# A graph-attention layer on one core: shared adjacency and key buffers, weight-row terms as columns, five x buffers

## The chip, the cores and the metric

The kernel runs on one core of a Trainium2 chip. It is one program: TensorE (PE in the profile), VectorE (DVE), ScalarE (ACT), GpSimd (POOL) and SyncE (SP, which here only issues DMAs) each run their own list of instructions in order and wait for each other through semaphores. The metric is the device time of one execution in microseconds (us). Lower is better.

## The reference

The inputs are x (3327 rows of 1024 fp32), a symmetric 0/1 matrix adj (3327 x 3327, int32, with ones on the diagonal, some 0.5% of its entries set), weights Wf, Wg, W (1024 x 1024) and biases bf, bg, bW (1024, zeros in this data but computed with).

```python
h = jnp.maximum(_layernorm(x, axis=-1), 0.0)
f = h @ Wf + bf
g = h @ Wg + bg
e = jax.nn.relu(f @ g.T)
scores = jnp.where(adj > 0, e, NEG)
attention = jax.nn.softmax(scores, axis=1)
out = x + attention @ (h @ W + bW)
```

(The reference's lines, with the inner function written in place.) Only the scores at the entries of adj that are set matter.

## The kernel before, in words

The kernel works on edges instead of the full matrix (function `edge_path`). If a row turns out to have too many edges, it falls back on a dense version (`dense_path`), which doesn't run on this data.

It uses e(i, j) = relu(q(i) · h(j) + q(i, D)), where q = h A + v, A = Wf Wg^T, v is the row bf Wg^T, column D of A is Wf bg, and element D of v is bf · bg. All of A, v and bW3 must be there before the second part can end its first product.

**Part 1** (L369 to L606) loops over 26 tiles of 128 rows (the last has 127). For each tile t:

- `degrees(t)` loads 128 rows of adj into `a` (1.7 MB, sync queue, L446), takes Relu on ACT with the row sum as degree (L448) into `r`, and multiplies `r` by the column number on POOL (L449). `a` and `r` have two buffers each (L376, L377), of 13.3 KB in each partition.
- `normed(t)` loads x (L417, sync queue, buffer `xt` from a pool of three, L374), computes mean and variance (on DVE for odd t, on ACT for even t), normalizes, takes Relu on ACT (L438) and stores h to a DRAM table `hd` (L440, ACT's queue).
- `edges(t, r)` finds the column numbers of the set entries on DVE: sixteen max8 instructions over segments of r (L458), then five more max8 with replacement (L465, L467), and writes the list and the degree to `pay`. PE counts degrees in a running histogram `pre` (L476, L481), from which DVE reads the rank of each row among those of its degree (`hit`, L478).
- for t below 8, `load_Wg(t)` loads 128 rows of Wg and transposes them on PE (L498, L499) into WgT; for t from 8 to 15, `make_A(t - 8)` loads rows of Wf, transposes them, and multiplies them with WgT on PE (L525, 32 instructions for each c), with copies out of PSUM on ACT (L528) and one column for Wf bg (L531, L532).

After the loop, rows are ranked by degree (L562 to L600), which gives `perm`: row numbers in order of falling degree. Then `make_rows` (L601) computes v on PE as rows of three equal copies (L543, from bf3, three copies of bf as columns), and `split3` turns v, and bW loaded three times as a row (`bWf`), into three bf16 terms that sum to it, one in each of three partitions. It does so on DVE over [3, 512] tiles: for each of the five pieces a copy (L355), three roundings (L359), three multiplications with a row of the 3 x 3 identity `sel3` (L361, L363), two subtractions (L365) and a copy (L366). The results v3 and bW3 are added later by a bf16 product with `ones3`.

**Part 2** goes through the 26 tiles of sorted rows. `prepare(s)` gathers the lists (`pi`) and h rows (`hp`) by perm (POOL queue, L627), transposes hp on PE (L638), and computes q on PE (L655, with v3 added in L656) and ACT (L657). `dot` gathers one neighbour row G of hd for each of 128 rows and dots it with q on DVE (L672); `softmax`, `combine` (L729 to L735) and `project` (L749, with bW3 added in L750) follow, and `finish` scatters the result. The G buffers, W_sb (4 MB, L610), pi and others use SBUF memory that part 1 gives back.

The order of instructions on each engine and queue isn't the program's. A planner orders them when the program is built, by its own estimates of durations, by the order of the program as a priority, and by when a buffer comes free. On the chip each engine keeps to that order and waits.

Of the kernel before, what the change touches and what calls it, by code (L numbers as in the profile page):

```python
# [8 lines left out]
FP = mybir.dt.float32  # L9
I32 = mybir.dt.int32  # L10
AF = mybir.ActivationFunctionType
ALU = mybir.AluOpType
# [7 lines left out]
BF = mybir.dt.bfloat16  # L20
SEG = 16
# [267 lines left out]
def edge_path(ctx: ExitStack, tc: tile.TileContext, x, adj, Wf, bf, Wg, bg, W, bW, out, flag):  # L289
# [10 lines left out]
    nc = tc.nc  # L300
    N, D = x.shape
    O = W.shape[1]
    P = 128
    CB = 512
    KD = D // P
    QB = 342
    QW = 3 * QB
    NT = (N + P - 1) // P
    OH = O // CB
    SW = -(-N // SEG)  # L310
    PW = KM + 1

    def rows(t):
        return min(P, N - t * P)

    def pieces(t):

        n = rows(t)
        m = n - n % 16
        return [(0, m), (m, n - m)] if 0 < m < n else [(0, n)]  # L320

    const = ctx.enter_context(tc.tile_pool(name="const", bufs=1))
# [5 lines left out]
    ident = const.tile([P, P], FP, name="ident")  # L328
# [4 lines left out]
    nc.gpsimd.iota(iotak, pattern=[[1, KM]], base=0, channel_multiplier=0, allow_small_or_imprecise_dtypes=True)  # L333
    ones3 = const.tile([3, P], BF, name="ones3")
    nc.gpsimd.memset(ones3, 1.0)
    sel3 = const.tile([3, 3], FP, name="sel3")
    make_identity(nc, sel3)
    bads = const.tile([P, NT + 2], FP, name="bads")
    nc.gpsimd.memset(bads, 0.0)

# [5 lines left out]
    v3 = wts.tile([3, QW], BF, name="v3")  # L346
    nc.gpsimd.memset(A_sb[:, :, D:], 0.0)
    nc.gpsimd.memset(v3[:, D:], 0.0)
    bW3 = wts.tile([3, O], BF, name="bW3")

    def split3(pool, to, of):

        n = of.shape[1]
        rest = pool.tile([3, n], FP, name="rest")
        tc.keep_in_program_order(nc.vector.tensor_copy(rest, of))  # L355
        part = pool.tile([3, n], BF, name="part")
        acc = pool.tile([3, n], FP, name="part_acc")
        for i in range(3):
            nc.vector.tensor_copy(part, rest)  # L359
            if i == 0:  # L360
                nc.vector.tensor_scalar(acc, part, sel3[:, 0:1], None, op0=ALU.mult)  # L361
            else:
                nc.vector.scalar_tensor_tensor(acc, part, sel3[:, i : i + 1], acc, op0=ALU.mult, op1=ALU.add)  # L363
            if i < 2:
                nc.vector.tensor_sub(rest, rest, part)  # L365
        nc.vector.tensor_copy(to, acc)  # L366


    with ExitStack() as part1:  # L369
        pool1 = lambda name, bufs, **kw: part1.enter_context(tc.tile_pool(name=name, bufs=bufs, **kw))  # L370
        c1 = pool1("c1", 1)
        wrow = pool1("wrow", 2)
        wT = pool1("wT", 2)
        ln = pool1("ln", 3)  # L374
        lnj = pool1("lnj", 1)
        apool = pool1("adj", 2)  # L376
        kpool = pool1("key", 2)  # L377
        cpool = pool1("cand", 2)
        p_tr = pool1("p_tr", 2, space=PSUM)
        p_mm = pool1("p_mm", 2, space=PSUM)  # L380
        p_u = pool1("p_u", 1, space=PSUM)
# [3 lines left out]
        iotaj = c1.tile([P, N], FP, name="iotaj")  # L385
# [6 lines left out]
        part = c1.tile([P, 1], FP, name="part_no")  # L392
# [6 lines left out]
        nc.gpsimd.memset(onesd, 1.0)  # L399
        pay = c1.tile([P, NT, PW], I32, name="pay")  # L400
        deg = c1.tile([P, NT], FP, name="deg")
        cnt = c1.tile([P, NT], FP, name="cnt")
        rp = c1.tile([P, NT], FP, name="rp")
        oh = c1.tile([P, NT, NBIN], BF, name="oh")
# [36 lines left out]

        def degrees(t):
            n = rows(t)
            a = apool.tile([P, N], I32, name="a")
            for b, m in pieces(t):
                nc.sync.dma_start(a[b : b + m], adj[t * P + b : t * P + b + m, :])  # L446
            r = kpool.tile([P, N], FP, name="r")
            nc.scalar.activation(r[:n], a[:n], AF.Relu, accum_out=deg[:n, t : t + 1])  # L448
            nc.gpsimd.tensor_mul(r[:n], r[:n], iotaj[:n])  # L449
            return r  # L450

        def edges(t, r):
# [30 lines left out]
        def store_lists(t0, t1):  # L483
            full = min(t1, N // P)
            if full > t0:
                nc.scalar.dma_start(
                    pd[t0 * P : full * P, :].rearrange("(t p) k -> p t k", p=P), pay[:, t0:full, :]
                )
            if t1 > full:
                for b, m in pieces(full):  # L490
                    nc.scalar.dma_start(pd[full * P + b : full * P + b + m, :], pay[b : b + m, full, :])

        def transposed(to, of):

            for g in range(0, KD, 4):
                ps = p_tr.tile([P, 4, P], FP, name="ps_tr")
                for k in range(4):
                    nc.tensor.transpose(ps[:, k, :], of[:, (g + k) * P : (g + k + 1) * P], ident)  # L498
                nc.scalar.copy(to[:, g : g + 4, :], ps)  # L499

        WgT = c1.tile([P, KD, D], FP, name="WgT")
        bfT = c1.tile([P, KD], FP, name="bfT")
        bgT = c1.tile([P, KD], FP, name="bgT")
        bf3 = c1.tile([P, KD, 3], FP, name="bf3")
        bWf = c1.tile([3, O], FP, name="bWf")
        nc.gpsimd.dma_start(bfT, bf.rearrange("(k p) -> p k", p=P))
        nc.gpsimd.dma_start(bgT, bg.rearrange("(k p) -> p k", p=P))
        nc.gpsimd.dma_start(bWf, bass.AP(tensor=bW.tensor, offset=bW.offset, ap=[[0, 3], [1, O]]))
        nc.vector.tensor_copy(bf3, bfT[:, :, None].to_broadcast([P, KD, 3]))

        def load_Wg(c):
            wr = wrow.tile([P, D], FP, name="wr")
            nc.sync.dma_start(wr, Wg[c * P : (c + 1) * P, :])
            transposed(WgT[:, :, c * P : (c + 1) * P], wr)

        def make_A(c):

            wr = wrow.tile([P, D], FP, name="wr")
            nc.sync.dma_start(wr, Wf[c * P : (c + 1) * P, :])
            WfT = wT.tile([P, KD, P], FP, name="WfT")  # L520
            transposed(WfT, wr)
            for o in range(OH):
                ps = p_mm.tile([P, CB], FP, name="ps_A")
                for k in range(KD):
                    nc.tensor.matmul(  # L525
                        ps, WfT[:, k, :], WgT[:, k, o * CB : (o + 1) * CB], start=(k == 0), stop=(k == KD - 1)
                    )
                nc.scalar.copy(A_sb[:, c, o * CB : (o + 1) * CB], ps)  # L528
            ps = p_u.tile([P, P], FP, name="ps_u")
            for k in range(KD):  # L530
                nc.tensor.matmul(ps[:, 0:1], WfT[:, k, :], bgT[:, k : k + 1], start=(k == 0), stop=(k == KD - 1))  # L531
            nc.scalar.copy(A_sb[:, c, D : D + 1], ps[:, 0:1])  # L532

        def make_rows():

            ps = p_u.tile([P, P], FP, name="ps_u")
            for k in range(KD):
                nc.tensor.matmul(ps[:3, 0:1], bf3[:, k, :], bgT[:, k : k + 1], start=(k == 0), stop=(k == KD - 1))
            split3(c1, v3[:, D : D + 1], ps[:3, 0:1])
            for o in range(OH):  # L540
                ps = p_mm.tile([P, CB], FP, name="ps_A")
                for k in range(KD):
                    nc.tensor.matmul(  # L543
                        ps[:3], bf3[:, k, :], WgT[:, k, o * CB : (o + 1) * CB], start=(k == 0), stop=(k == KD - 1)
                    )
                split3(c1, v3[:, o * CB : (o + 1) * CB], ps[:3])
                split3(c1, bW3[:, o * CB : (o + 1) * CB], bWf[:, o * CB : (o + 1) * CB])

        for t in range(NT):
            r = degrees(t)  # L550
            normed(t)
            edges(t, r)
            if t % 4 == 3 and t > 4:
                store_lists(t - 7, t - 3)
            if t < KD:
                load_Wg(t)
            elif t < 2 * KD:
                make_A(t - KD)
        store_lists(20, NT)


# [27 lines left out]
        ps = p_u.tile([P, P], FP, name="ps_u")  # L589
        for t in range(NT):  # L590
            nc.tensor.matmul(
                ps[:, : 2 * NT], ohp[:, t, :], place[:, t, :, :].rearrange("p a s -> p (a s)"),
                start=(t == 0), stop=(t == NT - 1),
# [4 lines left out]
        over = c1.tile([P, 1], FP, name="over")  # L598
        nc.vector.tensor_scalar(over, part, float(rows(NT - 1)), float(N), op0=ALU.is_ge, op1=ALU.mult)
        nc.vector.tensor_tensor(final, perm[:, NT - 1 : NT], over, op=ALU.add)  # L600
        make_rows()  # L601
        ne = c1.tile([P, NT], FP, name="ne")
        nc.vector.tensor_tensor(ne, deg, cnt, op=ALU.not_equal)
        nc.vector.tensor_reduce(bads[:, NT : NT + 1], ne, AX.X, ALU.max)
# [176 lines left out]
    for s, cap in enumerate(CAPS):  # L781
        half = (cap + 1) // 2
# [11 lines left out]
    for i, (s, k0, k1) in enumerate(units):  # L794
# [5 lines left out]
        if i + 1 < len(units):  # L800
            s2, a, b = units[i + 1]
# [12 lines left out]
def kernel(tc: tile.TileContext, x, adj, Wf, bf, Wg, bg, W, bW, out):  # L814

    nc = tc.nc
    with tc.tile_pool(name="flag", bufs=1) as fpool:
        flag = fpool.tile([1, 1], I32, name="flag")  # L820
        bad = edge_path(tc, x, adj, Wf, bf, Wg, bg, W, bW, out, flag)
        with tc.If(bad > 0):
            dense_path(tc, x, adj, Wf, bf, Wg, bg, W, bW, out)
# [27 lines left out]
```

## Time and profile before

| what | us |
|---|---|
| median of 3 runs | 1439.14 (1438.37 to 1440.06) |
| the profiled execution | 1437.97 |
| its span, first to last instruction | 1436.2 |
| busy in the span: DVE | 1266.7 (88%) |
| PE, matmuls | 1160.7 (81%) |
| POOL | 873.6 (61%) |
| ACT | 442.7 (31%) |

The mean granted TensorE clock was 0.927 of full speed, and DMA moved 259 GB/s on average. Times in the profile are counted from the start of the span. A busy share is an average over stages with different limits, so stages have to be looked at one by one. L12 is line 12 of the kernel. A line with `A <- B` in a list of waits says that A's engine stood idle until B ended. A line of the timeline has the start, the duration, the engine, the line, the operation, what is written and read, and, in square brackets, how long the engine was idle before it and who ended that.

### The profile page before, as it was taken

How to read it: one execution, taken by the hardware profiler on the slowest of the kernel's cores; microseconds unless marked ns; L12 is line 12 of the kernel's file. 1: busy time of each engine (PE TensorE's matmuls, PEld its weight loads, DVE VectorE, ACT ScalarE, POOL GpSimd, SP SyncE). 2: the span in 40 equal slices, each digit the busy share in tenths (PEclk: the TensorE clock that was granted, in tenths of full speed). 3: DMA queues.
4: the chain of work that ended last, by engine and by line, in shares of the span. 5: the costliest groups of instructions: out<-in, count | busy, mean ns of one | idle time of the engine just before them, and what ended most of it. 6: DMA issues, size and time to landing. Idle time of an engine off the chain costs nothing.

```text
span 1436.2 us, 13878 instructions
## 1 busy us (share of the span) xinstructions
PE 1160.7 (81%) x4242; PEld 657.3 (46%) x4242; DVE 1266.7 (88%) x2647; ACT 442.7 (31%) x673; POOL 873.6 (61%) x627
## 2 busy tenths in 40 slices
PE   1249899457087998999979888999999998999676
PEld 1225454034063665556455444555555554555332
DVE  3878888977979999998988889999999988999991
ACT  6666757301060444324122221222222111111100
POOL 8676776426756677665575556666676765666500
PEclk9999899769588999999989898999999998999788
DMA  8898887249768888896796668887787776787700
GB/s 340 292 348 294 325 302 260 86 140 402 236 224 310 310 315 276 302 314 206 279 324 210 230 261 281 292 286 271 266 287 258 257 254 228 252 275 256 263 30 32
DMA packets 97709, 372.51 MB, mean 259 GB/s; under 512 B 14265, under 2 KB 14681, under 8 KB 94297
## 3 DMA queue, kind: packets, MB, share of 16 engines
q0 software_dynamic: 79552, 286.86, 57.6%
q1 hardware_dynamic: 10860, 70.49, 13.4%
q10 hardware_dynamic: 7212, 14.18, 2.6%
q8 instruction: 35, 0.57, 0.2%
q14 instruction: 50, 0.41, 0.1%
HBM read 343.68 MB, written 27.80 MB: 259 GB/s over the span
## 4 chain that ended last, share of the span: by engine, by line
PE 35%; DVE 27%; issue 18%; POOL 10%; DMA 6%; ACT 3%; POOLq 0%; ACTq 0%; SPq 0%; DVEq 0%
PE ps_o L749 16%; DVE y L735 12%; PE ps_q L655 10%; POOL r L449 6%; DVE junk L672 5%; PE yT_ps L713 5%; DMA G<-hd,pi 4%; POOL G L627 4%; DVE cand L458 3%; PE ps_A L525 2%; ACT r L448 1%; PE ps_A L543 1%; DVE xp L757 1%; DVE sc L672 1%; DVE lst L465 1%
## 5 line engine op out<-in xcount | busy, mean ns | idle before, releaser
L627 POOL DMA_INDIRECT G<-hd,pi x468 | 560.8, 1198 | 316.6 <-ACT y L733 99.1
L672 DVE CUSTOM_DVE_ANT_0 junk<-G,q 128x1024 bf16<-128x1024 f32 x468 | 600.7, 1284 | 31.5 <-DMA G<-hd,pi 28.8
L655 PE MATMUL ps_q<-A_sb,hT 128*128 128x342 f32 x1248 | 394.5, 466 | 63.5 <-ACT q L657 53.5
L735 DVE SCALAR_TENSOR_TENSOR y<-G,sc,y 128x1024 f32<-128x1024 f32 x320 | 411.3, 1285 | 4.7 <-ACT y L733 2.9
L749 PE MATMUL ps_o<-W_sb,yT 128*128 128x512 f32 x832 | 387.1, 620 | 9.8 <-ACT yT L744 9.5
L655 PEld LDWEIGHTS ps_q<-A_sb,hT 128*128 128x128 f32 x1248 | 233.2, 194 | 183.4 <-ACT q L657 55.6
L749 PEld LDWEIGHTS ps_o<-W_sb,yT 128*128 128x128 f32 x832 | 161.0, 198 | 207.9 <-issue 189.1
L449 POOL TENSOR_TENSOR r<-r,iotaj 128x3327 f32<-128x3327 f32 (+1 forms) x26 | 187.8, 7232 | 73.1 <-ACT r L448 61.5
L458 DVE MAX8 cand<-r 128x8 f32<-128x208 f32 (+2 forms) x416 | 134.1, 361 | 39.8 <-POOL r L449 39.8
L657 ACT COPY q<-ps_q 128x342 f32<-128x342 f32 x78 | 32.8, 449 | 328.7 <-DVE sc L672 225.2
L729 ACT ACTIVATE G<-G,sc 128x1024 f32<-128x1024 f32 x122 | 129.0, 1136 | 0.0
L525 PE MATMUL ps_A<-WgT,WfT 128*128 128x512 f32 x256 | 120.3, 630 | 2.9 <-ACT WfT L499 2.9
L713 PE MATMUL yT_ps<-ident,G 128*128 128x128 f32 x976 | 116.4, 275 | 1.3 <-ACT G L729 1.3
L713 PEld LDWEIGHTS yT_ps<-ident,G 128*128 128x128 f32 x976 | 106.7, 141 | 13.2 <-ACT G L729 5.9
L639 ACT COPY hT<-ps_t 128x512 f32<-128x512 f32 x52 | 30.1, 593 | 192.1 <-PE ps_q L655 159.8
L744 ACT COPY yT<-yT_ps 128x512 f32<-128x512 f32 x52 | 27.8, 586 | 199.1 <-PE yT_ps L713 199.1
L525 PEld LDWEIGHTS ps_A<-WgT,WfT 128*128 128x128 f32 x256 | 50.8, 202 | 74.1 <-issue 64.7
L448 ACT ACTIVATE r<-a 128x3327 f32<-128x3327 int32 (+1 forms) x26 | 77.2, 2968 | 9.5 <-issue 5.4
L713 PE MATMUL yT_ps<-ident,y 128*128 128x128 f32 x208 | 33.8, 316 | 56.6 <-DVE y L735 35.7
L758 POOL DMA_INDIRECT out_dram<-xp,perm x25 | 31.7, 1268 | 56.9 <-DVE xp L757 50.9
L757 DVE TENSOR_TENSOR xp<-ps_o,xp 128x512 f32<-128x512 f32 x52 | 35.6, 685 | 34.2 <-PE ps_o L750 34.0
L713 PEld LDWEIGHTS yT_ps<-ident,y 128*128 128x128 f32 x208 | 28.0, 163 | 61.4 <-DVE y L735 38.5
(137 smaller groups left out, 748.7 us busy)
## 6 DMA issues: line engine op xcount, KB each, us to landing
a<-in_adj_dram SPq DMA_DIRECT2D x25, 1663.5 KB, 9.1
xt<-in_x_dram SPq DMA_DIRECT2D x25, 512.0 KB, 4.2
hd<-xt ACTq DMA_DIRECT2D x25, 512.0 KB, 5.6
G<-hd,pi POOLq DMA_INDIRECT x468, 6.1
wr<-in_L_gnn_Wg_dram SPq DMA_DIRECT2D x8, 512.0 KB, 6.0
wr<-in_L_gnn_Wf_dram SPq DMA_DIRECT2D x8, 512.0 KB, 5.0
W_sb<-in_L_gnn_W_dram SPq DMA_DIRECT2D x1, 4096.0 KB, 14.2
a<-in_adj_dram SPq DMA_DIRECT2D x1, 1455.6 KB, 9.6
```

Of the source, the lines that this page charges most:

```text
L448: nc.scalar.activation(r[:n], a[:n], AF.Relu, accum_out=deg[:n, t : t + 1])
L449: nc.gpsimd.tensor_mul(r[:n], r[:n], iotaj[:n])
L458: nc.vector.max(cand[:n, s * 8 : s * 8 + 8], r[:n, s * SW : min(N, (s + 1) * SW)])
L525: nc.tensor.matmul(ps, WfT[:, k, :], WgT[:, k, o * CB : (o + 1) * CB], start=(k == 0), stop=(k == KD - 1))
L627: nc.gpsimd.indirect_dma_start(out=to, out_offset=None, in_=table, in_offset=bass.IndirectOffsetOnAxis(ap=idx, axis=0),)
L655: nc.tensor.matmul(ps[:, :QB], hT[:, k, :], A_sb[:, k, o : o + QB], start=(k == 0), stop=False)
L672: nc.vector.tensor_tensor_reduce(junk, g, e["q"][:, :D], 1.0, e["q"][:, D : D + 1], op0=ALU.mult, op1=ALU.add, accum_out=e["sc"][:, k : k ...
L713: nc.tensor.matmul(e["yT"][:, c, :], g[:, c * P : (c + 1) * P], ident, is_transpose=True, start=(first and c % 4 == 0), stop=(last and c % ...
L729: nc.scalar.activation(g, g, AF.Copy, scale=p)
L735: nc.vector.scalar_tensor_tensor(y, g, p, y, op0=ALU.mult, op1=ALU.add)
L749: nc.tensor.matmul(ps, yT[:, k, :], W_sb[:, k, o * CB : (o + 1) * CB], start=(k == 0), stop=False)
L757: nc.vector.tensor_add(xo, e["o"][o], xo)
```

## The change

There are five edits.

1. `a` and `r` become one tile: adj is loaded as int32 into a tile `r` of a pool with four buffers, Relu on ACT works in place (the same bytes read as int32 and written as fp32), and the product on POOL follows in place.
2. For the last two tiles Relu and the product work on the columns in two parts, with the second row sum in `half`, added by an Identity on ACT.
3. `split3`, `sel3`, `bf3` and `bWf` go. v is computed as eight columns of 128 (WgT chunks as the stationary operand, bf as a moving column), bW is loaded as eight columns of 128, and bf · bg makes a seventeenth. They are split into three bf16 terms as a [128, 17] tile on DVE, and PE turns each column's three terms into a three-partition row by a product with a bf16 identity (16 products of 128 columns and one of one column). ACT copies the rows out of PSUM.
4. `make_rows` is called inside the loop, after the tile t = 9 and its make_A, not after the ranking.
5. The pool of `xt` (and its small tiles) has five buffers instead of three.

```diff
-        ln = pool1("ln", 3)
+        ln = pool1("ln", 5)
...
-        apool = pool1("adj", 2)
-        kpool = pool1("key", 2)
+        kpool = pool1("key", 4)
...
         def degrees(t):
             n = rows(t)
-            a = apool.tile([P, N], I32, name="a")
+            r = kpool.tile([P, N], FP, name="r")
+            a = r.bitcast(I32)
             for b, m in pieces(t):
                 nc.sync.dma_start(a[b : b + m], adj[t * P + b : t * P + b + m, :])
-            r = kpool.tile([P, N], FP, name="r")
-            nc.scalar.activation(r[:n], a[:n], AF.Relu, accum_out=deg[:n, t : t + 1])
-            nc.gpsimd.tensor_mul(r[:n], r[:n], iotaj[:n])
+
+            cuts = [0, SEG // 2 * SW, N] if t >= NT - 2 else [0, N]
+            for i, (b, e) in enumerate(zip(cuts, cuts[1:])):
+                to = deg[:n, t : t + 1] if not i else half[:n]
+                nc.scalar.activation(r[:n, b:e], a[:n, b:e], AF.Relu, accum_out=to)
+                nc.gpsimd.tensor_mul(r[:n, b:e], r[:n, b:e], iotaj[:n, b:e])
+                if i:
+                    nc.scalar.activation(deg[:n, t : t + 1], deg[:n, t : t + 1], AF.Identity, bias=half[:n])
             return r
...
-        bf3 = c1.tile([P, KD, 3], FP, name="bf3")
-        bWf = c1.tile([3, O], FP, name="bWf")
+        cols = c1.tile([P, 2 * KD + 1], FP, name="cols")
+        terms = c1.tile([P, 3, 2 * KD + 1], BF, name="terms")
+        identb = c1.tile([P, P], BF, name="identb")
+        nc.vector.tensor_copy(identb, ident)
+        nc.gpsimd.memset(cols, 0.0)
...
-        nc.gpsimd.dma_start(bWf, bass.AP(tensor=bW.tensor, offset=bW.offset, ap=[[0, 3], [1, O]]))
-        nc.vector.tensor_copy(bf3, bfT[:, :, None].to_broadcast([P, KD, 3]))
+        nc.gpsimd.dma_start(cols[:, KD : 2 * KD], bW.rearrange("(k p) -> p k", p=P))
...
         def make_rows():
             ps = p_u.tile([P, P], FP, name="ps_u")
-            ...
+            for c in range(KD):
                 for k in range(KD):
                     nc.tensor.matmul(
+                        ps[:, c : c + 1], WgT[:, k, c * P : (c + 1) * P], bfT[:, k : k + 1],
+                        start=(k == 0), stop=(k == KD - 1),
                     )
+            for k in range(KD):
+                nc.tensor.matmul(ps[0:1, KD : KD + 1], bfT[:, k : k + 1], bgT[:, k : k + 1], start=(k == 0), stop=(k == KD - 1))
+            nc.scalar.copy(cols[:, :KD], ps[:, :KD])
+            nc.scalar.copy(cols[0:1, 2 * KD :], ps[0:1, KD : KD + 1])
+            for i in range(3):
+                nc.vector.tensor_copy(terms[:, i, :], cols)
+                if i < 2:
+                    nc.vector.tensor_sub(cols, cols, terms[:, i, :])
+            for row, first in ((v3, 0), (bW3, KD)):
+                for o in range(OH):
+                    ps = p_mm.tile([P, CB], FP, name="ps_A")
+                    for k in range(CB // P):
+                        c = first + o * (CB // P) + k
+                        nc.tensor.matmul(ps[:3, k * P : (k + 1) * P], terms[:, :, c], identb, start=True, stop=True)
+                    nc.scalar.copy(row[:, o * CB : (o + 1) * CB], ps[:3])
+            ps = p_u.tile([P, P], FP, name="ps_u")
+            nc.tensor.matmul(ps[:3, 0:1], terms[:, :, 2 * KD], identb[:, 0:1], start=True, stop=True)
+            nc.scalar.copy(v3[:, D : D + 1], ps[:3, 0:1])
 
         for t in range(NT):
...
             elif t < 2 * KD:
                 make_A(t - KD)
+            if t == KD + 1:
+                make_rows()
         store_lists(20, NT)
...
-        make_rows()
```

More of the change, by code (lines that the diff above doesn't have):

```diff
@@ L335, in edge_path @@
     nc.gpsimd.memset(ones3, 1.0)
-    sel3 = const.tile([3, 3], FP, name="sel3")
-    make_identity(nc, sel3)
     bads = const.tile([P, NT + 2], FP, name="bads")
@@ L349, in edge_path @@
     bW3 = wts.tile([3, O], BF, name="bW3")
[L351 to L366, printed above, removed]
     with ExitStack() as part1:
@@ L401, in edge_path @@
         deg = c1.tile([P, NT], FP, name="deg")
+        half = c1.tile([P, 1], FP, name="half")
         cnt = c1.tile([P, NT], FP, name="cnt")
@@ L536, in make_rows @@
             ps = p_u.tile([P, P], FP, name="ps_u")
[L537 to L541, printed above, removed]
+            for c in range(KD):
                 for k in range(KD):
                     nc.tensor.matmul(
-                        ps[:3], bf3[:, k, :], WgT[:, k, o * CB : (o + 1) * CB], start=(k == 0), stop=(k == KD - 1)
-                    )
-                split3(c1, v3[:, o * CB : (o + 1) * CB], ps[:3])
-                split3(c1, bW3[:, o * CB : (o + 1) * CB], bWf[:, o * CB : (o + 1) * CB])
+                        ps[:, c : c + 1], WgT[:, k, c * P : (c + 1) * P], bfT[:, k : k + 1],
+                        start=(k == 0), stop=(k == KD - 1),
+                    )
+            for k in range(KD):
[16 more added lines that the diff above has]
+            nc.scalar.copy(v3[:, D : D + 1], ps[:3, 0:1])
         for t in range(NT):
```

## The prediction

> **What bounds the kernel now.** The span by stages comes first (columns: us, busy us of PE, PEld, DVE, ACT, POOL with counts, clock, DMA share, GB/s). The stages are mine: weights Wg (0 to 93), the eight make_A (93 to 250), last tiles, ranking, hand-over, main part.
>
> ```profile
> core 0: us, PE busy (x) PEld busy (x) DVE busy (x) ACT busy (x) POOL busy (x), PEclk, DMA share, GB/s
> 0.00:93.00 93.00, 20.20 (x86) 15.92 (x87) 62.80 (x306) 60.67 (x86) 68.11 (x38) 1.00 0.87 326
> 93.00:250.00 157.00, 142.05 (x466) 73.69 (x466) 126.67 (x628) 105.67 (x160) 111.32 (x16) 0.96 0.81 299
> 250.00:277.00 27.00, 18.30 (x44) 3.09 (x43) 22.11 (x109) 12.67 (x22) 16.56 (x3) 0.80 0.41 119
> 277.00:291.00 14.00, 1.60 (x31) 1.28 (x31) 12.59 (x34) 0.00 (x0) 0.00 (x0) 0.50 0.06 18
> 291.00:330.00 39.00, 25.22 (x99) 15.95 (x98) 24.11 (x60) 3.58 (x7) 14.18 (x15) 0.75 0.56 203
> 330.00:1436.00 1106.00, 953.36 (x3522) 547.40 (x3521) 1018.38 (x1513) 260.11 (x400) 663.43 (x558) 0.93 0.74 257
> ```
>
> The main part is VectorE's: 1018 of 1106 us. The change doesn't touch it, so what comes before it moves the end one for one. Before it no engine is full, except PE from 93 to 250, with 142 of 157. So I asked for the waits of the first 330 us (total us, times, longest), the sync queue's own and then all.
>
> ```profile
> SPq L417 <- DMA hd<-xt: 147.3, 18, 15.9
> SPq L610 <- DMA pd<-pay: 32.6, 1, 32.6
> SPq L610 <- DVE bW L366: 24.7, 1, 24.7
> ```
>
> ```profile
> POOL r L449 <- ACT r L448: 61.5, 18, 8.1
> ...
> ACT nmr L437 <- DVE rstd L436: 30.1, 11, 4.7
> ```
>
> The sync queue stood 147 us because a load of x wanted one of three buffers whose store to hd had not landed; adj and weight loads stood behind it. POOL waited 61 us for ACT's Relu, which itself stood behind small statistics that wait on DVE. The timeline shows the hand-over.
>
> ```profile
> 291.63 1.08 POOL L627 DMA_INDIRECT hp<-hd,perm  x1 [21.90 <-DVE rest L355]
> ...
> 304.95 1.94 PE L638 MATMUL ps_t<-ident,hp 128*128 128x128 f32 x8 [13.49 <-DVE rest L355]
> ...
> 306.76 6.84 PE L655 MATMUL ps_q<-A_sb,hT 128*128 128x342 f32 x16
> ...
> 315.58 0.95 POOL L627 DMA_INDIRECT pi<-pd,perm  x1 [7.13 <-DVE bW L366]
> ...
> 323.97 0.45 ACT L657 COPY q<-ps_q 128x342 f32<-128x342 f32 x1 [4.60 <-PE ps_q L656]
> ...
> 329.88 1.28 DVE L672 CUSTOM_DVE_ANT_0 junk<-G,q 128x1024 bf16<-128x1024 f32 x1 [5.93 <-DMA G<-hd,pi]
> ```
>
> perm is known at 290.8 (L597 runs from 290.59 for 0.18), yet split3 holds DVE from 291.5 to 315.3. PE's first transposes wait for its last read of PSUM (rest L355), the lists (pi) and W_sb for its end. The first dot starts 39.1 us after perm.
>
> **What the Trainium skill says.** "TensorE: Matmul & The Clock Gate", Architectural detail: ACT and DVE are strict FIFO, PE reorders only weight loads; the ACT wait above agrees. Same page, What's actually happening: an idle PE runs at half clock for its first few us; the first 16 matmuls of q took 6.84 us here, the next 4.87. "DMA: Bandwidth & Descriptors", Issuing engines are not separate DMA queues: all queues share 16 engines, so earlier W_sb competes with the gathers; with W_sb under way, gathered G took 8.8 us to land in the first 330 us against 6.1 over the span. "ScalarE: Activation LUTs", Table sets: cheap functions such as identity are in every set; so the new Identity should load no table. The trace has loads for Sqrt at 15.4 and Exp at 342.2 and none between, though Relu, Copy and Square run there; it has no Identity.
>
> **The change, part by part.**
> *split3 leaves the hand-over.* Removed from DVE: 291.5 to 315.3, 23.8 us. What is late next? hp is issued at perm plus 0.9, or 2.1 if a pi goes first (1.25 each); landing 4.8 (median of its three); transposes to first q matmul 1.8 (304.95 to 306.76); q to its last copy 17.7 (306.76 to 324.42). Sum 25.2 to 26.4; W_sb's 4 MB beside it may add up to 6 us, a warm PE may take 2 off. I take 26. G is not later: pi lands after about 6 (5.8), G is issued then and takes 8.8: 16 to 17. By the first dot, 7 or more lie ready, so the 1.1 us gap after the first dot goes too. Gain 39.1 - 26 + 1 = **14 us** (bounds 8 to 16).
> *make_rows at t = 9.* PE loses L543, 17.4 us, and L538, 0.55, all but 0.26 of it after 249.7, beside the last tiles. It gains 8 x 8 column products, each two instructions: L531 makes 16 in 1.84, so 128 take 14.7; bf·bg 0.55 to 1.84; 17 one-pass bf16 products at 0.1 to 0.24 (L476 takes 0.19 to 0.24), 2 to 4. Sum 17 to 21, now ahead of make_A(2) on PE and in p_u and p_mm. ACT gains three copies at 0.16 and four at 0.56, 2.7 us; DVE three casts and two subtracts of 17 columns at about 0.17, 0.85, and one 128x128 cast. The handing over PE, ACT, DVE, PE is in order: ACT may be in a Relu (2.97), DVE in sixteen max8 (5.8). Nothing bounds a gap below 0 if PE has make_A work queued in between; at most it is about 22, as worked out under the rivals. I take 3.
> *Small loads.* bW as columns goes on POOL's queue like bgT (0.96 to issue, 7.4 to land); POOL's first product waits for ACT until 13.3, so nothing. sel3, bf3 and bWf go: under 1 us, hidden by the first adj load.
> *Four shared buffers, five for x.* Before, r lived from Relu through POOL to the last max8: 3.0 + 7.2 + 5.8 plus handing over and interleaved work, about 20 us for two buffers: a tile each 10 us, as POOL shows ((262.5 - 13.3) / 25 = 10.0). Now a buffer also holds the load (9.1): 25 to 30 us over four, 6.3 to 7.5 a tile. The wait of adj load t + 4 on max8 of t is new; behind it on the sync queue stand x and weight loads, with slack while tiles take over 7.5 us. The x wait needs a store that lags five tiles instead of three; I take it as gone.
> What bounds the loop then? DVE: 62.8 + 126.7 + 22.1 = 212 busy from 13.3 on: 225. DMA: 30.3 + 46.9 + 3.2 = 80 MB (GB/s times us) at 351 GB/s, the best 30 us stretch here: 229, and 3 + 7.2 + 6 for the last tile: 245. PE: the first make_A starts about 88 instead of 94 (the DMA share of 0.87 can rise), 142 us of work, 17 of make_rows, 3 of gap, 5 of waits (15 before): 255, and the last tile's ranking 2. PE is the largest: the loop ends at **257** instead of 277, gain 20. Bounds: 0 (tiles stay in step with make_A) and 32.
> *Last two tiles in halves.* DVE could start on tile 25 up to 5.1 us earlier, half of POOL's 7.2 and of Relu's 3. It was busy until 270.8 anyway; 0 to 5, inside the 20. The Identity costs ACT 0.3 twice; it is behind the Relu, under POOL's second half; uncovered it would cost 0.3 of the 20.
>
> Sum: 257 + 14 (ranking) + 26 + 1105 (main part less the gap) = 1402 span. The profiled execution took 1437.97 against its span of 1436.2, 1.8 more, and the median of the runs 1.2 more still: **1405 us**, that is 34 less.
>
> **The rivals.**
> *Hand-over only.* Two tiles went with each make_A (19.4 us), and ACT waited 14.3 us for ps_A to copy. If the new order keeps that step, PE sets the pace, the rows' 17 us trade places with L543's 17.4, and the loop still ends near 277. Gain 14, and 2 for the halves: 1423. For it: PE's 142 of 157. Against: PE also waited on DVE, and the wait on x is gone.
> *Better still.* If tiles run ahead of make_A and gaps in PE's first 93 us (73 idle) fill, DMA sets the end: 245. Gain 32 + 14: 1393.
> *Slower: the rows stall PE.* At t = 9 PE stands for cols on ACT and terms on DVE (3 + 5.8), then four times for p_mm's two buffers to be copied behind a Relu (3 each): with 1.3 in semaphores 22, while tiles stay in step with make_A, so all of it lands in the loop. 22 - 14 = 8 more: 1447. From a stall of 14 us on this is a loss.
>
> **How the numbers follow.** Likeliest 0.55, its own range 1396 to 1416 (8 to 16 in the hand-over, 15 to 27 in the loop); hand-over only 0.23; better still 0.12; slower 0.10. To hold 8 in 10 the range runs from 1391 to 1430, which takes in nearly all of the first two and half of the third. Within 0.2% (about what a measurement here can tell from no change, 3 us) lies only the edge between hand-over only and the stall, 0.02, taken from the slower case: faster 0.90, same 0.02, slower 0.08.
>
> **What would show it.** Right: first dot 25 to 28 us after perm, no DVE work between but a few checks; no long wait of x loads on hd; POOL's products less than 9.5 us apart; last make_A near 255 and no earlier than the column products allow. Wrong: pi or PE's first transpose still waiting on something other than perm or hp; PE idle over 10 us around the rows; adj loads waiting on max8; or DVE less busy in the main part than 92%, if the order there changed.

## The result and the profile after

The changed kernel is slower: 1450.33 us median of 4 runs (1449.28 to 1452.56), against 1439.49 (1438.37 to 1440.06) for the kernel before in the same comparison. The ratio is 1.0078, 95% interval 1.0061 to 1.0096. The forecast was 1405 us, with a range of 1391 to 1430. The profiled execution took 1449.28 us, its span 1447.4. One later batch, with three tiles ahead and with the first runs of three kernels that were then run again, fell on a slower chip, where the kernel before itself took 1502.71 us, so from it only ratios and times inside the loop are read.

The span by stages of the changed kernel, cut where its own stages end (columns as before: us, busy us of PE, PEld, DVE, ACT, POOL with counts, clock, DMA share, GB/s):

```profile
core 0: us, PE busy (x) PEld busy (x) DVE busy (x) ACT busy (x) POOL busy (x), PEclk, DMA share, GB/s
0.00:93.00 93.00, 20.29 (x86) 15.61 (x87) 66.58 (x307) 60.52 (x87) 68.39 (x37) 1.00 0.94 363
93.00:250.00 157.00, 142.69 (x530) 87.32 (x530) 106.31 (x528) 91.11 (x141) 93.46 (x14) 0.86 0.66 252
250.00:297.00 47.00, 31.16 (x110) 16.23 (x109) 43.52 (x220) 30.27 (x54) 34.92 (x7) 0.86 0.52 155
...
311.00:339.00 28.00, 18.89 (x65) 12.06 (x66) 0.88 (x7) 2.51 (x5) 17.57 (x19) 0.76 0.98 383
339.00:1447.00 1108.00, 962.17 (x3542) 552.14 (x3539) 1019.33 (x1516) 261.10 (x402) 657.01 (x554) 0.93 0.73 254
```

From 93 to 250 PE is busy for as long as before (142.7 us against 142.1), but DVE does 20 us less there, ACT 15 and POOL 18 less, and the granted clock is 0.86 instead of 0.96. That work is done later: the tiles now end near 297 instead of 277. The hand-over is shorter (28 us, with DVE all but idle) and the main part is about the same. Point by point:

| us from the start of the span | before | after |
|---|---|---|
| tile 12's product on POOL starts | 133.01 | 133.07 |
| tile 13's product starts | 140.2 | 167.82 |
| the last product ends | 269.73 | 291.18 |
| perm is ready | 290.77 | 310.56 |
| first dot starts | 329.88 | 338.94 |
| span | 1436.2 | 1447.4 |

(POOL's two products of tiles 12 and 13 are one line in the trace of before, the second right behind the first:)

```profile
133.01 14.45 POOL L449 TENSOR_TENSOR r<-r,iotaj 128x3327 f32<-128x3327 f32 x2 [4.58 <-ACT r L448]
```

Up to tile 12 the two kernels run in step. Tile 13 is 27.6 us late, of which 6 are made up by the end of the loop. The hand-over then takes 28.4 us instead of 39.1, 10.7 less. 19.8 - 10.7 + 2.1 in the main part is the 11.2 us by which the span grew.

The waits of the first 330 us of the changed kernel (engine, line, what ended the wait: total us, times, longest), the sync queue's own first:

```profile
SPq L508 <- PE pre L463: 60.0, 3, 27.1
SPq L428 <- DVE cand L445: 60.0, 10, 10.2
...
SPq L398 <- DMA hd<-xt: 32.3, 9, 11.2
```

```profile
POOL r L434 <- ACT r L433: 53.3, 13, 7.1
...
DVE hit L465 <- PE pre L463: 30.5, 7, 24.6
...
POOL r L434 <- DVE hit L465: 27.5, 1, 27.5
ACT nmr L418 <- DVE rstd L417: 26.5, 11, 4.3
ACT cols L534 <- PE ps_u L533: 25.3, 1, 25.3
```

The load of x waits 32 us for a store to hd, where it waited 147: most of the wait is gone, as predicted of edit 5. In its place adj loads (L428) wait 60 us for the last max8 of an old tile, the wait that the shared buffers add. POOL's wait for Relu is still 53 us, that of the small statistics 26.5. New are three long waits of 24.6 to 27.5 us on DVE, ACT and POOL, and the timeline shows that they are one event. The changed kernel around tile 13:

```profile
135.00 25.62 PE L528 MATMUL ps_u<-bfT,WgT 128*128 128x1 f32 x128
...
161.02 0.23 PE L463 MATMUL pre<-oh,tri 128*128 128x64 bf16 x1
...
161.12 0.17 ACT L534 COPY cols<-ps_u 128x8 f32<-128x8 f32 x1 [25.34 <-PE ps_u L533]
...
161.29 0.23 DVE L465 SCALAR_TENSOR_TENSOR hit<-pre,oh 128x64 f32<-128x64 f32 x1 [24.55 <-PE pre L463]
...
164.69 2.97 ACT L433 ACTIVATE r<-r 128x3327 f32<-128x3327 int32 x1
...
167.82 7.23 POOL L434 TENSOR_TENSOR r<-r,iotaj 128x3327 f32<-128x3327 f32 x1 [27.52 <-DVE hit L465]
```

make_rows' 64 column products stand on PE as one block without a gap. Each is two instructions (the trace has 128), and all take 25.62 us. Behind them on PE stands one histogram product (L463), 0.23 us long, which has nothing to do with them. DVE's hit waits for that product, and DVE's max8 stand behind hit. ACT waits in the copy to cols, and the Relu of tile 13 stands behind that copy. So POOL gets no tile for 27.5 us: one block on PE stopped the three other engines. It stopped the loads as well: the next load of Wf (L508) needs a buffer that transposes behind the block read, and it waits 27.1 us on the sync queue, with the loads of x and adj behind it. From 142 to 158 the DMA engines moved nothing. (The wait of L434 is put down to hit, which ended at 161.5; the Relu on ACT, from 164.69 to 167.66, ended last.)

The block is longer than 128 times the price of before because the clock fell under it. First before's products with one column (L531), then stretches of PE alone in the changed kernel (us, PE busy, clock, DMA share, GB/s):

```profile
131.42 1.84 PE L531 MATMUL ps_u<-bgT,WfT 128*128 128x1 f32 x16
```

```profile
131.00:135.00 4.00, 3.33 (x29) 1.00 0.24 99
...
136.00:137.00 1.00, 1.00 (x10) 0.92 1.09 98
137.00:138.00 1.00, 1.00 (x6) 0.50 0.68 213
138.00:141.00 3.00, 3.00 (x16) 0.50 0.99 399
```

A mean of 0.92 from 136 to 137 puts the fall from 1.00 to 0.50 at about 136.8, 1.8 us into the block, and the clock stays at 0.50 to the block's end, though the profile shows PE busy throughout. On average an instruction of the block takes 25.62 / 128 = 0.200 us instead of the 1.84 / 16 = 0.115 of before's L531. The next make_A begins at that clock: 16.41 us for its 32 instructions at 169.50, where the one at 117.62 took 14.00.

The hand-over of the changed kernel:

```profile
310.38 0.18 DVE L601 SCALAR_TENSOR_TENSOR perm<-ps_u,tens 128x26 int32<-128x26 f32 x1
310.95 0.40 SPq L613 DMA_DIRECT2D W_sb<-in_L_gnn_W_dram  x1
311.40 1.07 POOL L630 DMA_INDIRECT hp<-hd,perm  x1 [20.21 <-DVE final L604]
312.77 0.98 POOL L630 DMA_INDIRECT pi<-pd,perm  x1 [0.30 <-issue]
...
320.11 1.94 PE L641 MATMUL ps_t<-ident,hp 128*128 128x128 f32 x8 [9.99 <-issue]
...
338.46 0.45 ACT L660 COPY q<-ps_q 128x342 f32<-128x342 f32 x1 [4.60 <-PE ps_q L659]
...
338.94 1.29 DVE L675 CUSTOM_DVE_ANT_0 junk<-G,q 128x1024 bf16<-128x1024 f32 x1 [17.43 <-ACT q L660]
```

hp is issued 0.84 us after perm and the lists right behind it, as predicted. PE's first transpose begins 8.7 us after hp's issue; W_sb's 4 MB load was issued 0.45 us before hp.

### The profile page after: what moved, and what is told of

It is laid out like the page before. It is cut to its first block, busy times and chain, and to the rows that moved or that the text cites. A ratio compares the mean times of both kernels' runs of the same rounds, so it can differ in the third digit from the quotient of the medians.

```text
span 1447.4 us, 14082 instructions
## 1 busy us (share of the span) xinstructions
PE 1176.7 (81%) x4355; PEld 684.5 (47%) x4355; DVE 1248.9 (86%) x2602; ACT 445.5 (31%) x686; POOL 871.4 (60%) x628
## 4 chain that ended last, share of the span: by engine, by line
PE 31%; DVE 25%; issue 20%; POOL 14%; DMA 7%; ACT 2%; POOLq 0%; SPq 0%; ACTq 0%; DVEq 0%
PE ps_o L752 15%; DVE y L738 13%; POOL r L434 8%; PE ps_q L658 6%; DVE junk L675 5%; POOL G L630 5%; DMA G<-hd,pi 4%; PE yT_ps L716 4%; PE ps_A L514 3%; DVE cand L445 2%; PE ps_u L528 2%; DMA pi<-pd,perm 1%; DVE xp L760 1%; ACT G L732 1%; DVE sc L675 1%
## 5 line engine op out<-in xcount | busy, mean ns | idle before, releaser
L434 POOL TENSOR_TENSOR r<-r,iotaj 128x3327 f32<-128x3327 f32 (+4 forms) x28 | 188.4, 6742 | 93.8 <-ACT r L433 53.3
L433 ACT ACTIVATE r<-r 128x3327 f32<-128x3327 int32 (+4 forms) x28 | 77.5, 2768 | 0.6 <-ACT xt L419 0.5
L760 DVE TENSOR_TENSOR xp<-ps_o,xp 128x512 f32<-128x512 f32 x52 | 35.6, 685 | 35.7 <-PE ps_o L753 35.4
L716 PEld LDWEIGHTS yT_ps<-ident,y 128*128 128x128 f32 x208 | 28.7, 166 | 62.3 <-DVE y L738 39.3
```

The source lines that it names most:

```text
L433: nc.scalar.activation(r[:n, b:e], a[:n, b:e], AF.Relu, accum_out=to)
L434: nc.gpsimd.tensor_mul(r[:n, b:e], r[:n, b:e], iotaj[:n, b:e])
L716: nc.tensor.matmul(e["yT"][:, c, :], g[:, c * P : (c + 1) * P], ident, is_transpose=True, start=(first and c % 4 == 0), stop=(last and c % ...
L760: nc.vector.tensor_add(xo, e["o"][o], xo)
```

## The experiments

Four theories were on the table. *Block*: the column products (128 instructions) in one block, with everything that stands behind them in order, are the loss. *Hand-offs*: it is the chain cols, terms, rows between the engines, wherever the products are. *Buffers*: the shared buffers with their new wait cost time themselves. *Order*: the planned order on ACT, not the buffers, sets the tiles' pace, so that the buffers have little to give. All ratios are to the kernel before, with 95% intervals. Times inside a run, such as perm, are those of one profiled execution: two kernels below with the same loop have perm at 292.3 and 295.4, so differences of up to 3 us between single profiles are not resolved.

**Each half of the change alone.** The first kernel is the kernel before with edits 1, 2 and 5, and with make_rows and split3 as they were (`degrees` as in the change, cut here):

```diff
-        ln = pool1("ln", 3)
+        ln = pool1("ln", 5)
...
-        apool = pool1("adj", 2)
-        kpool = pool1("key", 2)
+        kpool = pool1("key", 4)
...
```

> The kernel before with the shared four buffers, the two-part last tiles and five x buffers, but the old make_rows and split3 at their old place. Theory 1 (the loss is the row of column products at t = 9, and the buffers do nothing because ACT keeps the same order for tiles 0 to 12): 1433 to 1440 us, POOL's products at the same times as before up to tile 12, a gain of 0 to 6. Rival (the loss comes from the buffers, since an adj load now waits for max8 of four tiles back, 60 us of such waits): 1445 us or more.

Measured: 1430.16 us, ratio 0.9951 (0.9936 to 0.9966). Tiles 0 to 12 are where they were (tile 12's product at 133.00 against 133.01); the last product ends at 264.13 instead of 269.73, perm is ready at 284.19. So the buffers cost nothing: they give 8 us, 2 more than was expected of them, and only late in the loop. The halves of the last two tiles (edit 2) are in this kernel too, but the product of tile 23, the last whole one, already starts at 239.73 instead of 244.94, so most of the gain is there before them. POOL's wait for Relu over the first 330 us fell from 61.5 to 36.8, but part of it is now put down to DVE: all its waits before these products went from 73.1 to 66.9 only.

The second is the changed kernel with edits 3 and 4 alone, on the buffers of before (`degrees` as before, cut here):

```diff
-        ln = pool1("ln", 5)
+        ln = pool1("ln", 3)
...
-        kpool = pool1("key", 4)
+        apool = pool1("adj", 2)
+        kpool = pool1("key", 2)
...
```

> The kernel before with only the column form of the rows at t = 9; two and two buffers, three x buffers. Theory 1: the stall of some 27 us is there, 1447 to 1456 us. Rival (buffers): the hand-over's gain of 11 is left without the loss, 1426 to 1430 us.

Measured: 1457.11 us, ratio 1.0121 (1.0093 to 1.0149), perm at 313.54. The time is 1 us over the range of the first theory, and the hole is there in full, with two and two buffers. Tile 13 in the timeline of this kernel:

```profile
167.93 7.24 POOL L430 TENSOR_TENSOR r<-r,iotaj 128x3327 f32<-128x3327 f32 x1 [27.58 <-DVE hit L459]
```

The loss belongs to the new make_rows in its place at t = 9, and the theory *buffers* is out.

**A shorter block in the same place.** Only the first of the eight products of each column is issued, which leaves 16 of the 128 instructions. v is incomplete by this; all hand-offs stay.

```diff
-                for k in range(KD):
+                for k in range(1):
...
-                        start=(k == 0), stop=(k == KD - 1),
+                        start=True, stop=True,
```

> The changed kernel with 16 column products instead of 128: only the first of eight parts of each sum is taken, so v is left incomplete (bf is zero in the data). All else as in the changed kernel. Theory 1: the block shrinks from 26 to about 3 us, the hole in POOL's products after tile 12 from 27.5 to under 8, and the time by 20 to 25, to 1425 to 1430 us. Rival: 1445 us or more.

Measured: 1433.07 us, ratio 0.9956 (0.9941 to 0.9970), perm at 293.22: 17.3 us earlier for 112 instructions fewer, which on PE are 25.62 - 1.84 = 23.8. The time is 3 to 8 us over what was expected, and the timeline of this kernel says why:

```profile
136.87 1.84 PE L528 MATMUL ps_u<-bfT,WgT 128*128 128x1 f32 x16
...
143.44 1.05 ACT L546 CAST v<-ps_A 3x512 bf16<-3x512 f32 x2 [3.53 <-PE ps_A L545]
...
150.84 7.25 POOL L434 TENSOR_TENSOR r<-r,iotaj 128x3327 f32<-128x3327 f32 x1 [9.37 <-ACT r L433]
```

Sixteen of the instructions are back at 0.115 each. But ACT stands 2.06 us before the copy to cols and 3.53 before the copies of the rows, then does those, and the Relu only after them: POOL's hole is still 9.4 us, where under 8 was expected. So both theories, *block* and *hand-offs*, have a part: the block about 17 us, and the hand-offs, as the timeline suggests, the rest. Against the kernel with the buffers alone (perm at 284.19), the changed kernel's perm at 310.56 is 26.4 us late, 17.3 from the 112 instructions and 9.0 from what stays without them.

**The block spread out.** All 128 instructions, sixteen at a time. In the first kernel they stand in load_Wg(c), t below 8, in PE's idle first 93 us, with the rest of make_rows after t = 7 instead of 9:

```diff
         def load_Wg(c):
...
+            for k in range(KD):
+                nc.tensor.matmul(
+                    psv[:, c : c + 1], WgT[:, k, c * P : (c + 1) * P], bfT[:, k : k + 1],
+                    start=(k == 0), stop=(k == KD - 1),
+                )
...
-            if t == KD + 1:
+            if t == KD - 1:
                 make_rows()
```

> The changed kernel with the sixteen products of each column issued right after the transposes of its chunk of Wg, for t below 8, where PE is 78% idle, and the rest of make_rows after t = 7. Theory 1: no hole in POOL's products, 1420 to 1430 us. Rival: 1445 us or more. A third case, that a block of 16 one-column products (3.2 us at half clock) still delays a histogram product each time: 1430 to 1440 us.

Measured: 1432.08 us, ratio 0.9964 (0.9951 to 0.9976), perm at 292.27, first dot 27.6 us later. This is 2 us over the range of the first theory and inside that of the third case, but the third case's reason isn't there: DVE's hit waits for PE 6.7 us in all, before 7.8. All the work of the change is in, and the block's 17 us are gone: the time is that of the shortened block within 1 us, so in this place the 112 further instructions cost nothing that shows. What is left against the buffers alone is 8.1 us at perm, about as much as with the short block, though the hand-offs now come two tiles earlier. A sixteen takes 3.6 us here:

```profile
20.78 3.58 PE L507 MATMUL ps_u<-bfT,WgT 128*128 128x1 f32 x16
```

That is the slow price, 0.22 us each, and eight transposes take 1.94 us here (1.07 at 115.62 in the changed kernel, at a clock of 1.00). Yet the view gives a clock of 1.00 for all of the first 93 us. The durations and the view don't agree there, so the clock of 1.00 in that stage should not be relied on.

In the second they stand in make_A(c), t from 8 to 15, after its own column, and the rest of make_rows after t = 15:

```diff
         def make_A(c):
...
+            for k in range(KD):
+                nc.tensor.matmul(
+                    psv[:, c : c + 1], WgT[:, k, c * P : (c + 1) * P], bfT[:, k : k + 1],
+                    start=(k == 0), stop=(k == KD - 1),
+                )
...
-            if t == KD + 1:
+            if t == 2 * KD - 1:
                 make_rows()
```

> The changed kernel with the sixteen products of one column of v issued inside each make_A, after its own sixteen products with bg, and the rest of make_rows after t = 15. The products' price: if a run of one-column products is cheap while PE is warm, each sixteen take 1.84 us as L531's do, 14.7 in all, against 25.6 in one block. No hole in POOL's products of over 10 us. Theory that a block ahead of Relu's queue was the loss: 1427 to 1437 us, like the spread over the Wg stage. Theory that PE is the pace from 93 to 250 us, as the prediction had it: 12 to 15 us more than the spread over the Wg stage.

Measured: 1441.03 us, ratio 1.0011 (0.9998 to 1.0024), perm at 301.04, 9 us after that of the kernel with load_Wg. PE in this kernel:

```profile
116.29 2.37 PE L525 MATMUL ps_u<-bfT,WgT 128*128 128x1 f32 x16
...
120.88 15.73 PE L516 MATMUL ps_A<-WgT,WfT 128*128 128x512 f32 x32
```

The second sixteen in a row take 1.93 us in six of the eight places, and 2.37 and 2.79 in the other two. The clock falls under them as well (us, PE busy, clock, DMA share, GB/s):

```profile
117.00:118.00 1.00, 1.00 (x9) 0.80 0.00 0
118.00:119.00 1.00, 1.00 (x7) 0.50 0.00 0
```

All seven make_A behind such sixteens take 15.3 to 16.6; in the kernel with load_Wg three of those seven take 15.7 to 17.0 and four 14.0. From 93 to 260 PE is now busy for 159.7 of 167 us, there for 144.7. So where PE has little room, the same instructions cost 9 us even spread out. This is less than the 12 to 15 of the theory that PE is the pace, and more than the other theory allows; and as the hand-offs moved as well, from t = 7 to t = 15, the 9 us are not the instructions' alone for certain.

**W_sb after the gathers.** The kernel with load_Wg, and the load of W_sb made to wait for the first q:

```diff
-    nc.sync.dma_start(W_sb, W.rearrange("(k p) o -> p k o", p=P))
...
     prepare(1)
+    nc.scalar.copy(W_sb[:, 0, 0:1], st[0]["q"][:, 0:1])
+    nc.sync.dma_start(W_sb, W.rearrange("(k p) o -> p k o", p=P))
```

> The spread version with the 4 MB load of W_sb held until the first q is done (a one-column copy of q into W_sb, then overwritten, makes it wait). Theory 3 (the load, now beside the first gathers, makes hp land after 8.7 us instead of 4.8): hp lands in 4 to 5 us, the first dot comes 3 to 4 us sooner after perm, 1 to 4 us less than the spread version. Rival: the load then costs the same in the first G gathers, and the time doesn't change.

Measured: 1432.72 us, ratio 0.9959 (0.9946 to 0.9972). hp is there 4.6 us after its issue instead of 8.4, and the first dot is 24.4 us after perm instead of 27.6. But the median is that of the same kernel with the early load, within 0.7 us, so the rival is right about the time. In the profiled executions the main part took 1115.6 us instead of 1109.4 (this one was 4.5 us over its median). That W_sb's load delays hp is shown; the 3 us won don't reach the end, and where they go wasn't followed further.

**Tiles further ahead.** If the order is what holds the tiles, then the order of the program has to change, since it is the planner's priority. The spread kernel, with degrees called one and two tiles ahead of normed and edges (here two):

```diff
+        keys = {t: degrees(t) for t in range(2)}
         for t in range(NT):
-            r = degrees(t)
+            if t + 2 < NT:
+                keys[t + 2] = degrees(t + 2)
             normed(t)
-            edges(t, r)
+            edges(t, keys.pop(t))
```

> The spread version, and degrees (adj load, Relu, product on POOL) of tile t + 1 put into the program ahead of the statistics and the list of tile t, so that ACT's planned order has Relu ahead of the statistics that wait for DVE. Theory 2 (tiles were slow because of the order on ACT, not for lack of buffers): POOL's idle time in the loop falls from some 70 us to under 35, perm comes 15 to 30 us earlier, 1400 to 1417 us. Rival (PE or DVE is the bound of the loop all the same): within 6 us of the spread version.

Measured: 1414.61 us, ratio 0.9841 (0.9799 to 0.9883), perm at 273.87. The time is in the range, but POOL's idle time before its products fell from 72.0 us to 56.1 only.

> The same with degrees two tiles ahead. Theory 2: as with one tile ahead or up to 5 us faster; if loads in four buffers then come too late for each other, slower than one ahead.

Measured: 1400.17 us, ratio 0.9741 (0.9701 to 0.9780), perm at 260.53, and POOL's idle time 38.1. That is 14 us below one tile ahead, where 5 at most were expected. This is the fastest kernel here, 50 us below the changed one. Its waits of the first 275 us:

```profile
POOL r L434 <- ACT r L433: 33.6, 16, 6.6
...
DVE cand L445 <- POOL r L434: 9.1, 3, 6.1
```

In the spread kernel these were 55.4 and 35.4, and ACT's wait for rstd fell from 25.2 to 7.7. No buffer was added and no work taken out, so with these buffers the order was what held the tiles. make_A now ends at 233.5 (before 249.7). Its stage and the stretch from there to perm:

```profile
93.00:233.50 140.50, 136.22 (x476) 71.99 (x474) 126.11 (x625) 107.15 (x170) 114.03 (x18) 1.00 0.87 316
233.50:260.50 27.00, 3.30 (x41) 2.00 (x38) 25.34 (x103) 9.68 (x21) 2.33 (x1) 0.56 0.26 86
```

PE is busy for 97% of the first, so now PE does set the pace there; the second is DVE's.

A third tile ahead:

> The spread version with degrees three tiles ahead instead of two. With four buffers, three tiles ahead leave one in work: no gain over two ahead, 1397 to 1408 us; if POOL's remaining idle time is still ACT's order, 5 to 10 us less.

Measured: ratio 0.9799 (0.9748 to 0.9850), perm at 264.5: no sooner than with two.

**How much of this is the order alone?** Two tiles ahead in the kernel before, in the kernel with the buffers alone, and in the changed kernel itself (same diff of the loop as above). All three ran first in the batch on the slower chip (the e10, e11 and e12 of the texts below), with ratios of 0.9875 (0.9788 to 0.9962), 0.9861 (0.9801 to 0.9920) and 0.9895 (0.9858 to 0.9933); these are the runs after it:

> As e10: the kernel before with degrees two tiles ahead and its own buffers. On the disturbed chip perm came at 283 us, 7.5 earlier than before. Needing the shared buffers: 1427 to 1434 us. Order alone enough: 1405 to 1413 us.

> As e11: shared buffers and old rows with degrees two tiles ahead. perm came at 261 us on the disturbed chip, as in the spread version with the same order. 1403 to 1412 us: perm 30 earlier than before, the long hand-over kept.

> As e12: the changed kernel with degrees two tiles ahead. perm came at 290 us on the disturbed chip. If the block still costs its 27 us: 1424 to 1432 us, with a hole of over 25 us in POOL's products.

| kernel, two ahead | median us | ratio (95%) | perm | first dot |
|---|---|---|---|---|
| before (2 + 2 buffers) | 1431.73 | 0.9937 (0.9891 to 0.9983) | 281.12 | 320.16 |
| buffers alone | 1410.58 | 0.9799 (0.9777 to 0.9821) | 263.61 | 302.91 |
| changed kernel | 1430.07 | 0.9935 (0.9915 to 0.9955) | 288.82 | 317.19 |
| spread rows (above) | 1400.17 | 0.9741 (0.9701 to 0.9780) | 260.53 | 288.82 |

All three times are in the ranges expected. The order alone gives 7.5 us, the buffers alone 8 (the kernel above), the two together 28.7: the buffers have room for tiles ahead, but only an order that runs ahead uses it. The new rows, spread over the Wg stage, give 10.4 more. As one block they cost 30 against that (1430.07 to 1400.17): in the changed kernel with tiles ahead the copy to cols still waits 24.1 us, DVE's hit 25.0, and POOL stands for 35.0 us at 132.5. Tiles that are ahead don't cover the block, since Relu and max8 stand behind it on ACT and DVE. Before the first of these runs one of two cases was that Relu, planned further ahead, keeps POOL fed and the hole shrinks to under 15 us; that case is out.

## Why the prediction was wrong, step by step

Predicted span 1402, measured 1447.4. Of these 45.4 us, 39.6 are in the loop (perm at 257 + 14 = 271 against 310.56), 2.4 in the hand-over (26 against 28.4) and 3.5 in the main part.

- **"make_rows at t = 9", the step that decides.** Its products were priced at 14.7 us from L531 and measured 25.6: L531's sixteen ran at a clock of 1.00, and the block spent all but its first 1.8 us at 0.50. The larger error is where the sum stood: "17 to 21, now ahead of make_A(2) on PE", as a term of PE's sum, with a gap of 3. What is queued behind the block was asked for the copies and terms, but not for PE's own queue, where the histogram product stands that DVE needs, nor for the copy to cols with the Relu behind it. So it was a stop of DVE, ACT and POOL as well. Measured by perm: 26.4 us on top of the kernel with the buffers alone. The sign named for such a stall, "PE idle over 10 us around the rows", looked at the wrong engine: PE was busy, and the engines that waited for it were idle.
- **"Four shared buffers, five for x": gain 20, of it 6.6 came** (perm 290.77 to 284.19). Most of the wait of x on hd went (147 us to 32), but it was not what held the tiles: up to tile 12 nothing moved. The waits on Relu and the statistics, read in the same view, were the ones that counted, and they fell once the order ran ahead as well. The rival "hand-over only" (0.23) had the buffers give nothing, but for another reason, that PE sets the pace.
- **PE as the bound of the loop at 255: not at this order.** With the products moved to where PE is idle, PE was the pace of its stage only once tiles ran two ahead; make_A then ended at 233.5 and perm came at 260.5, sooner than the 271 of the sum. At the order of the change PE was not the only pace, though not free either: with the products spread over the make_A stage it was busy for 96% of it, and perm came 9 us later.
- **"split3 leaves the hand-over": gain 14, measured 10.7**, inside its bounds of 8 to 16. The mis-sized term is hp's landing, 8.7 for 4.8, and W_sb's load is why, as the experiment with the late load shows. "W_sb's 4 MB beside it may add up to 6" was in the text, with nothing taken for it. The page "DMA: Bandwidth & Descriptors" of the Trainium skill (Issuing engines are not separate DMA queues) says that transfers started by different engines share the same 16 DMA engines; that was the right warning, and the trace agrees: 98% of the DMA engines' time, 383 GB/s over these 28 us.
- **The main part: right within 3.5 us**, 2.1 from before's. Over the other kernels without a change there it took 1103.6 to 1114.3 in the profiles, so 2 us can't be put down to the change.
- **The slower rival had the sign and nearly the size (1447 for 1450), in part by luck, since it set the loss at the wrong place.** It set 22 us for hand-offs cols, terms and p_mm's copies. The shortened block shows ACT's part of these, 2.06 + 3.53 us of standing and then the copies ahead of the Relu; what that kernel still loses at perm is about 9. The other 17 come from the block, which the rival didn't have. It was given 0.10, too little: that the engines run in order and that POOL already stood 61 us for ACT was in the views read.

What remains open: whether the 9 us left without the block are all hand-offs, what each of the edits 1, 2 and 5 gives alone, and where W_sb's 3 us go.

## What to carry to other kernels

Before a block of work is set into a loop, ask what stands behind it on its own engine, and who waits for that: the block stops each of those engines for its whole length, unless the engine has other work queued ahead of its wait. Split such a block into pieces and put them where the engine is idle: the same 128 instructions cost 17 us as a block, about 9 spread in the busy stage, and nothing that shows in the idle one. More buffers pay in full only with an order of work that uses them; here each alone gave 8 us, both together 29.

## What the hardware showed unexpectedly

- PE does not hold its clock on one-column fp32 products and transposes, though the profile shows it busy. In the changed kernel the clock fell from 1.00 to 0.50 at 136.8, 5.2 us after the last product of 512 columns had ended, and stayed there to the end of the block. An instruction then took 0.200 us on average instead of 0.115, and the dense make_A behind it 16.4 us instead of 14.0. With the old buffers the 128 took 25.70 us; with two tiles ahead, where the block began at 128.3, 24.42. Read in the same way, the fall came 2.9 to 5.6 us after the last product of 512 columns in the five kernels looked at, also behind the short block. DMA traffic isn't the reason, for in the kernel with the products in make_A it came at a DMA share of 0. What the reason is was not tested. It may be the single column or the transposes; and as bf and bg are zero in this data, the moving columns were all zeros too.
- The first gather of 128 rows of hd was there for PE 8.4 to 8.7 us after its issue beside a 4 MB load, and 4.6 us without it.
- With both under way the core moved 383 GB/s over 28 us.
